# Attention kernel, layer 1: the output projection by seven block products instead of eight, moved within the step

## The chip, the cores and the metric

The kernel runs on one core of one Trainium2 chip. The metric is the device time of one execution in microseconds (us), lower is better; it is given as the median of several executions. The engines are TensorE (PE in the profile, its weight loads PEld), VectorE (DVE), ScalarE (ACT), GpSimd (POOL) and the queue SyncE (SP) that issues the DMAs.

## The reference, cut to what matters

Two attention layers run one after the other over a picture `x` of 128 rows, 256 positions and 256 channels, each with a residual addition. The change concerns layer 1 alone, and in it the last line but one:

```python
# layer 1: x2 is the group-normed picture, one row of 256 positions at a time
qkv = x2 @ w_in.T + b_in                       # 256 -> 768 channels
q, k, v = jnp.split(qkv, 3, axis=-1)           # 4 heads of 64
scores = jnp.einsum('bhid,bhjd->bhij', q, k) / sqrt(64)
scores = jnp.where(|i - j| <= 16, scores, -inf)
attn = softmax(scores)
out = jnp.einsum('bhij,bhjd->bhid', attn, v)
y = out @ w_out.T + b_out                      # the output projection, 256 -> 256
x = x + y
```

## The kernel before

Layer 0 takes the first 1975 us of the profiled execution, layer 1 the rest. Both take the rows in 64 pairs. In layer 1 a pair is an object of class `Pair1`, and one pass of the loop over `p` (L2203) is a step. The order of all work is written out by hand in that loop: each call puts its instructions on the queues of the engines in just this order, and an engine executes its queue in order. A step works on several pairs at once: `now` is pair p, `was` the pair before, `nxt`, `nn` and `n3` are the next three, so that their loads, normalisation and projections run ahead of their attention.

What happens to a pair, with the names that the steps of the prediction use:

- Its rows come from memory in two forms: `xs` for the transposed picture and `xt` for the residual (L1923, L1928, issued on SP three steps ahead). `turn` transposes on DVE (L1936), `centre(k)` normalises on ACT, one call for each of the two halves of the channels (L1941), `add_bias` adds the output bias to `xt` on POOL (L1947).
- Q, K and V of a pair (n = 0, 1, 2) are each a product of two 2 x 2 block matrices: the channels are two halves of 128, and the two rows of the pair are the other index. It is computed by seven block products instead of eight. `mix_weights` forms four combinations of the weight blocks once (L1904 to L1907), `differences` four combinations of the data blocks of each pair on POOL (L1954 to L1957). `product(n, i)` is one of the seven, in the order 1, 2, 6, 5, 7, 4, 3 (L1968). Two PSUM accumulators serve them: x gets products 1, 6, 7, 4 one upon the other, and ACT copies x away after each of them (L1999 for V, L2001 for Q and K); y gets 2, then 5 and 3, and `join(n, i)` on DVE adds to y what ACT had copied (L2008). So a product that adds to x, or starts y anew, waits until x has been copied or y been joined. For V (n = 2) the data block is the stationary operand, and a product is two matmuls of 128 columns; for Q and K it is one matmul of 256.
- `scores(r)` of row r: 16 small matmuls, an exponential on ACT (L2054), and a multiplication by the band mask on POOL (L2056). `apply(r)` multiplies the result `e` by V (L2070) and by ones for the row sums (L2078), split into even and odd key blocks in separate accumulators.
- `copy_sums`, `copy_odd` (ACT, L2089, L2092) and `join_sums`, `join_odd` (DVE, L2095, L2098) bring even and odd together; `invert` takes the reciprocal of the sums (L2101), `weigh` multiplies (L2106) and leaves `oT`, the attention output of a row with channels on partitions; with row 1 it sends the inverted sums to memory (L2111).
- The output projection: `out_block(r, b)` multiplies one block of 128 positions of `oT` by both halves of the channels of `w_out` (L2124), 2 matmuls of 256 columns; a pair has 4 such blocks, 8 matmuls. They land in the second half of each of the two banks of `su_y`, whose first halves hold the row sums. `keep_row(r)` adds the residual `xt` on DVE, straight from PSUM (L2132), and with row 1 sends both rows out (L2140).
- Range checks: `look` queues two pieces for each stretch of 256 values, a maximum (L2160), and a comparison with a minimum (L2157, L2158), all on DVE. `some_checks(n)` takes n pieces from the queue. In most steps before there are two calls of one piece each.

The step before, in short: scores of both rows; application of row 1 of `was`; Q and K products 1, 2, 6, 5, 7; the projection of row 0 of `was`; Q and K products 4 and 3, for Q first, then for K; V products 1 and 2; application of row 0 of `now`; V products 6 and 5; half of the projection of row 1; V product 7; the other half; V products 4 and 3. The inversion and weighting of row 0, the second `centre`, `differences`, `add_bias` and the transposition stand at the end of the step.

```python
self.y = su_y[:, :, 1]
...
self.y[:, b], self.oT[r][:, k, b * P : (b + 1) * P], w_out[:, k, :],
start=(k == 0), stop=(k == KC - 1),
```

Of the kernel before, what the change touches and what calls it, by code (L numbers as in the profile page):

```python
# [9 lines left out]
F32 = mybir.dt.float32  # L10
# [6 lines left out]
P = 128  # L17
# [756 lines left out]
def fast_kernel(  # L774
# [1071 lines left out]
    with tc.tile_pool(name="l1", bufs=2) as sb, tc.tile_pool(  # L1846
# [19 lines left out]
        wst = sb.tile([P, 4, 3, P], F32, name="wst", bufs=1)  # L1866

# [43 lines left out]
        su_y = ps_o.tile([P, 2, 2, I], F32, name="ps_su_y1", tag="su")  # L1911
        su_eo = [su_y[:, n, 0] for n in range(2)]

        class Pair1:
# [53 lines left out]
            def product(self, n, i):  # L1968

                if len(self.ps) == n:  # L1970
                    self.ps.append([mm1("ps_qk", n % 2) for _ in range(2)])
                    self.u.append(sm.tile([P, 3, I], F32, name="u1", tag=f"u{n}", bufs=2))
# [88 lines left out]
            def apply(self, r):  # L2061


                e = self.es[r]
                gap = q0(2) - q0(0)
                for a in range(2):
                    for j in range(NK // 2):
                        for h in range(H1):
                            for k in (2 * j, 2 * j + 1):
                                nc.tensor.matmul(  # L2070
                                    o_eo[k % 2][h * DH : (h + 1) * DH, a, q0(k) : q0(k) + W],
                                    self.v[half(k), r, j, h * D1 + a * DH : h * D1 + (a + 1) * DH],
                                    e[half(k), h % 2, h // 2, j * W : (j + 1) * W], start=True, stop=True,
                                )
                for h in range(H1):
                    for n in range(2):
                        two = su_y[h * DH : (h + 1) * DH, n].rearrange("p a i -> p (a i)")
# [40 lines left out]
            def out_block(self, r, b):  # L2118
                if b == 0:
                    self.y = su_y[:, :, 1]  # L2120
                    if self.p == NP - 1:
                        self.y = mm1("ps_y1", r).rearrange("p (b c) -> p b c", b=NB)
                for k in range(KC):
                    nc.tensor.matmul(  # L2124
                        self.y[:, b], self.oT[r][:, k, b * P : (b + 1) * P], w_out[:, k, :],
                        start=(k == 0), stop=(k == KC - 1),
                    )

            def keep_row(self, r):
                if r == 0:  # L2130
                    self.yo = sb.tile([P, 2 * NB, C], F32, name="yo", tag="yo")
                nc.vector.tensor_tensor(  # L2132
                    self.yo[:, r * NB : (r + 1) * NB, :], self.y,
                    self.xt[:, r * NB : (r + 1) * NB, :], ALU.add,
                )
# [44 lines left out]
        with tc.manual_schedule():  # L2180
# [6 lines left out]
            for t in (*o_eo, su_y):  # L2187
# [14 lines left out]
            was = Nobody()  # L2202
            for p in range(NP - 1):  # L2203
# [14 lines left out]
                now.scores(1)  # L2218
                was.apply(1)
# [28 lines left out]
                nn.centre(0)  # L2248
                some_checks(2 if p > NP - LATE else 0)

                now.apply(0)
                now.copy_sums(0)
# [3 lines left out]
                now.copy_odd(0)  # L2256
                now.join_sums(0)
                was.out_block(1, 0)
                if fast:
                    nxt.product(2, 7)  # L2260
                now.join_odd(0)
                some_checks(2 if p > NP - LATE else p > 0)
                was.out_block(1, 1)
                if fast:
                    nxt.join(2, 5)
                was.keep_row(1)
                if fast:
                    nxt.product(2, 4)
# [4 lines left out]
                nn.centre(1)  # L2273
                nn.differences()
                nn.add_bias()
                n3.turn()
# [3 lines left out]
                was, now, nxt = now, nxt, nn  # L2280

            now.scores(0)
            was.apply(1)
# [106 lines left out]
```

## Time and profile before

| what | us |
|---|---|
| median of 3 executions (3117.92 to 3119.09) | 3118.25 |
| the profiled execution itself | 3119.44 |
| its span, from first to last instruction | 3117.7 |
| of which PE / DVE / ACT / POOL busy | 3016.7 / 2398.7 / 1574.1 / 2267.4 |
| L2124, output projection of layer 1, 1008 records, mean of one | 0.386 |
| L1988, V products, 744 records of the largest group, mean of one | 0.284 |
| L1992, Q and K products, 756 records of the largest group, mean of one | 0.379 |
| L1954, L1955, L1956 / L1957, data differences on POOL | 0.73 / 1.2 |
| L1947, bias addition on POOL, 1024 columns | 2.39 |
| L2132, residual addition on DVE, 512 columns | 0.685 |
| L2008, join on DVE | 0.42 |
| L1999, copy of V's x on ACT | 0.37 |

A group's row in the profile names line, engine and operation, the tiles written and read, shapes and count, then the time the engine was busy with the group and the mean of one in ns, then the idle time ahead of them and who ended it. Matmuls overlap: the mean of one is its latency, while the spacing of their starts says what one costs TensorE. The time line lists instructions in order of start, neighbours of one kind merged into one line with their count; the columns are the start from the span's beginning, the length, the engine, and in brackets, where there are any, the engine's idle time ahead and its releaser.

### The profile page before, as it was taken

The numbers are of one execution on the slowest core, as the hardware profiler recorded it, in microseconds if no ns is written. First come the engines' busy times: TensorE is split into PE (matmuls) and PEld (weight loads), VectorE is DVE, ScalarE is ACT, GpSimd is POOL, SyncE is SP. The second block draws the span as 40 slices with busy tenths as digits, with TensorE's granted clock in tenths as the row PEclk, the third lists the DMA queues.
The fourth block names the chain that finished last, engine by engine and source line by source line (L and its number), as shares of the span: only waits on it lengthen the run. The fifth ranks groups of instructions, "written<-read, shape, count | busy, mean of one in ns | idle before, by whom it ended". The sixth has DMA issues, their size and how long they took to land.

```text
span 3117.7 us, 80605 instructions
## 1 busy us (share of the span) xinstructions
PE 3016.7 (97%) x33642; PEld 2099.2 (67%) x33642; DVE 2398.7 (77%) x4010; ACT 1574.1 (50%) x2639; POOL 2267.4 (73%) x1636
## 2 busy tenths in 40 slices
PE   5689999999999999999999999999999999999998
PEld 4355555566555556555555655688888888888886
DVE  7987777777777777777777777688878777777788
ACT  3454444444444444444444444355555555555554
POOL 3469889889888989888998987455545555555553
PEclk9799999999999999999999999999999999999999
DMA  9952333323332332333233233443434343444431
GB/s 357 390 185 54 97 73 96 100 71 90 91 99 70 99 100 64 93 94 99 69 100 100 63 89 82 116 100 86 101 84 98 90 97 90 95 92 94 94 93 53
DMA packets 690775, 327.90 MB, mean 105 GB/s; under 512 B 538625, under 2 KB 639873, under 8 KB 689249
## 3 DMA queue, kind: packets, MB, share of 16 engines
q1 hardware_dynamic: 686000, 320.02, 38.6%
q8 instruction: 266, 4.36, 0.6%
q10 hardware_dynamic: 4400, 2.63, 0.3%
q14 instruction: 109, 0.88, 0.1%
HBM read 253.83 MB, written 68.74 MB: 103 GB/s over the span
## 4 chain that ended last, share of the span: by engine, by line
PE 91%; DMA 3%; DVE 3%; ACT 1%; POOL 1%; issue 1%; ACTq 0%; SPq 0%; DVEq 0%; POOLq 0%
PE ps_p L1364 21%; PE ps_qk L1992 12%; PE ps_sc L1401 9%; PE ps_ov L1436 7%; PE ps_su_y L2124 7%; PE ps_qk L1988 7%; PE ps_v L1382 7%; PE ps_y L1490 7%; PE ps_o L2070 4%; PE ps_su L1444 3%; PE ps_sc L2045 3%; PE ps_su_y L2078 2%; DMA xa<-in_x_dram 2%; DMA zt<-in_z_dram 1%; DVE st L1199 1%
## 5 line engine op out<-in xcount | busy, mean ns | idle before, releaser
L1425 POOL TENSOR_TENSOR eboth<-e 128x512 f32<-128x512 f32 x512 | 743.5, 1473 | 174.8 <-PE ps_su L1444 95.8
L1421 DVE TENSOR_TENSOR e<-ps_sc,eb 128x1024 f32<-128x1024 f32 x384 | 458.3, 1221 | 288.6 <-ACT ps_sc L1413 288.5
L1413 ACT ACTIVATE ps_sc<-ps_sc 128x1024 f32<-128x1024 f32 x384 | 375.4, 1007 | 435.5 <-PE ps_sc L1401 310.0
L1401 PE MATMUL ps_sc<-qT,kT 32*128 32x256 f32 x4096 | 294.0, 400 | 0.0
L1955 POOL TENSOR_TENSOR dT<-xgT,dT 128x256 f32<-128x256 f32 x63 | 45.9, 729 | 313.5 <-ACT xgT L1941 313.5
L2056 POOL TENSOR_TENSOR e<-e,bw 128x384 f32<-128x384 f32 x256 | 248.1, 1000 | 10.7 <-ACT e L2054 10.7
L2124 PE MATMUL ps_su_y<-w_out,oT 128*128 128x256 f32 x1008 | 254.5, 386 | 0.9 <-DVE sums L2095 0.9
L1401 PEld LDWEIGHTS ps_sc<-qT,kT 32*128 32x128 f32 x4096 | 185.6, 184 | 101.4 <-issue 93.0
L1490 PEld LDWEIGHTS ps_y<-wo,oT 128*128 128x128 f32 x1024 | 194.4, 190 | 81.6 <-issue 43.6
L1436 PE MATMUL ps_ov<-e,v 128*32 128x256 f32 x4096 | 247.6, 382 | 1.1 <-DVE v L1388 1.1
L1364 PE MATMUL ps_p<-xnT,wq 128*128 128x512 f32 x512 | 247.6, 606 | 0.1
L1364 PE MATMUL ps_p<-xgT,wg 128*128 128x512 f32 x512 | 247.3, 605 | 0.0
L1490 PE MATMUL ps_y<-wo,oT 128*128 128x256 f32 x1024 | 242.0, 380 | 1.7 <-POOL oT L1480 1.7
L1382 PE MATMUL ps_v<-wv,xnT 128*128 128x256 f32 x1024 | 241.9, 379 | 0.0
L1364 PE MATMUL ps_p<-xnT,wk 128*128 128x512 f32 x512 | 240.7, 593 | 0.0
L1382 PEld LDWEIGHTS ps_v<-wv,xnT 128*128 128x128 f32 x1024 | 194.6, 190 | 53.9 <-issue 30.9
L2101 DVE RECIPROCAL rv<-sums 128x256 f32<-128x256 f32 x128 | 223.1, 1743 | 0.0
L2001 ACT ACTIVATE u<-ps_qk,bin_c 128x256 f32<-128x256 f32 x378 | 174.3, 475 | 95.0 <-PE ps_qk L1992 95.0
L2124 PEld LDWEIGHTS ps_su_y<-w_out,oT 128*128 128x128 f32 x1008 | 181.9, 190 | 22.3 <-DVE sums L2095 1.3
L1436 PEld LDWEIGHTS ps_ov<-e,v 128*32 128x32 f32 x4096 | 120.2, 110 | 109.2 <-issue 41.4
L1954 POOL TENSOR_TENSOR dT<-xgT 128x256 f32<-128x256 f32 x63 | 46.0, 730 | 184.8 <-ACT xgT L1941 184.8
L1364 PEld LDWEIGHTS ps_p<-xnT,wk 128*128 128x128 f32 x512 | 97.3, 190 | 122.7 <-issue 122.5
(234 smaller groups left out, 6607.1 us busy)
## 6 DMA issues: line engine op xcount, KB each, us to landing
xa<-in_x_dram SPq DMA_DIRECT2D x8, 4096.0 KB
xt<-in_x_dram SPq DMA_DIRECT2D x64, 512.0 KB
x<-xo SPq DMA_DIRECT2D x16, 2048.0 KB
xt<-x SPq DMA_DIRECT2D x64, 512.0 KB
rvb<-rsum SPq DMA_DIRECT2D x252, 128.0 KB
xs<-x SPq DMA_DIRECT2D x252, 128.0 KB
out_dram<-yo SPq DMA_DIRECT2D x63, 512.0 KB
xs<-in_x_dram SPq DMA_DIRECT2D x248, 128.0 KB
```

The source lines that it names most:

```text
L1364: nc.tensor.matmul(ps, w[:, k, m * P : (m + 1) * P], getattr(self, src)[:, k, :], start=(k == 0), stop=(k == KC - 1),)
L1382: nc.tensor.matmul(self.ps_v[:, b * C : (b + 1) * C], self.xnT[:, k, t * P : (t + 1) * P], wv[:, k, :], start=(k == 0), stop=(k == KC - 1),)
L1401: nc.tensor.matmul(self.pss[q // 2][:, q % 2, b, :], self.kT[rs, c, r * I + b * P : r * I + (b + 1) * P], self.qT[rs, c, r * I : (r + 1) * I],
L1413: nc.scalar.activation(self.pss[a], ps, AF.Exp)
L1421: nc.vector.tensor_tensor(es[a], pss[a], eb[:, h : h + 2], ALU.mult)
L1425: nc.gpsimd.tensor_tensor(t, es[a][:, :, 0, :], es[a][:, :, 1, :], ALU.add)
L1436: nc.tensor.matmul(ov[q * D0 : (q + 1) * D0, c, :], self.v[:, r, b, h * D0 : (h + 1) * D0], es[q // 2][:, q % 2, b, :], start=(b == 0), st ...
L1490: nc.tensor.matmul(self.ps_y[:, b * C : (b + 1) * C], self.oT[r][:, k, b * P : (b + 1) * P], wo[:, k, :], start=(k == 0), stop=(k == KC - 1),)
L1992: nc.tensor.matmul(to, lhs, rhs, start=start, stop=True, skip_group_check=True)
L2056: nc.gpsimd.tensor_tensor(e[:, q], e[:, q], bcast(bw.rearrange("p b w -> p (b w)"), 1, KC), ALU.mult)
L2101: nc.vector.reciprocal(self.rv[:, r, :], self.sums)
L2124: nc.tensor.matmul(self.y[:, b], self.oT[r][:, k, b * P : (b + 1) * P], w_out[:, k, :], start=(k == 0), stop=(k == KC - 1),)
```

## The change

- `out_block`'s 8 matmuls of a pair become seven block products of two matmuls of 128 columns each, by the same scheme as Q, K and V: `mix_weights` forms four combinations `wso` of the blocks of `w_out` once, `row_sums` four combinations `oS` of the blocks of `oT` per pair on POOL, `out_product(i)` is a product, with a copy on ACT after 1, 6, 7 and 4 (into `uy`, for 4 straight into the output tile `yo`), `out_join(i)` a join on DVE after 2, 5 and 3. The accumulators are the second halves of two banks, now two tiles.
- The residual is no longer added from PSUM on DVE: `keep_rows` adds `xt` to the whole of `yo` on POOL, one step later (as `old`, two pairs behind `now`), and then sends both rows out.
- The order of the step: all Q and K products 1, 2, 6, 5, 7 run on, and the application of row 0 follows them; then Q and K products 4, 4, 3, 3, then V's seven and the output's seven interleaved in one run. `join_odd(1)` stands ahead of `invert(1)`. The transposition `n3.turn`, `centre(1)`, `differences` and `add_bias` move from the end of the step into or ahead of that run.
- Both pieces of the range checks stand after the last output join, ahead of `invert(0)` and `weigh(0)`; in the late steps two more stand after `row_sums`.
- The buffers `u` of the products go from two to one. The last pair and the one before it keep the old projection; for the one before it the residual addition is split in two.

```diff
+        wso = sb.tile([P, 4, P], F32, name="wso", bufs=1)
...
+            a = [[w_out[:, k, m * P : (m + 1) * P] for k in range(KC)] for m in range(KC)]
+            s1, s2, s3, s4 = (wso[:, n] for n in range(4))
+            nc.gpsimd.tensor_tensor(s1, a[1][0], a[1][1], ALU.add)
+            nc.gpsimd.tensor_tensor(s2, s1, a[0][0], ALU.subtract)
+            nc.gpsimd.tensor_tensor(s3, a[0][0], a[1][0], ALU.subtract)
+            nc.gpsimd.tensor_tensor(s4, a[0][1], s2, ALU.subtract)
...
-        su_y = ps_o.tile([P, 2, 2, I], F32, name="ps_su_y1", tag="su")
-        su_eo = [su_y[:, n, 0] for n in range(2)]
+        su_y = [ps_o.tile([P, 2, I], F32, name=f"ps_su_y{n}", tag=f"su{n}") for n in range(2)]
+        su_eo = [t[:, 0] for t in su_y]
...
+            def row_sums(self):
+
+                self.oS = sb.tile([P, 4, I], F32, name="oS1", tag="oS", bufs=1)
+                b = [[self.oT[r][:, k, :] for r in range(2)] for k in range(KC)]
+                t1, t2, t3, t4 = (self.oS[:, n] for n in range(4))
+                nc.gpsimd.tensor_tensor(t1, b[0][1], b[0][0], ALU.subtract)
+                nc.gpsimd.tensor_tensor(t2, b[1][1], t1, ALU.subtract)
+                nc.gpsimd.tensor_tensor(t3, b[1][1], b[0][1], ALU.subtract)
+                nc.gpsimd.tensor_tensor(t4, b[1][0], t2, ALU.subtract)
+
+            def quarter(self, m, r):
+                return self.yo[:, r * NB : (r + 1) * NB, m * P : (m + 1) * P]
+
+            def out_product(self, i):
+
+                if i == 1:
+                    self.yo = sb.tile([P, 2 * NB, C], F32, name="yo", tag="yo")
+                    self.uy = sm.tile([P, 3, I], F32, name="uy1", tag="uy", bufs=1)
+                x, y = (t[:, 1] for t in su_y)
+                w = lambda m, k: w_out[:, k, m * P : (m + 1) * P]
+                b = lambda k, r: self.oT[r][:, k, :]
+                to, rhs, lhs, start = {
+                    1: (x, w(0, 0), b(0, 0), True),
+                    2: (y, w(0, 1), b(1, 0), True),
+                    6: (x, wso[:, 1], self.oS[:, 1], False),
+                    5: (y, wso[:, 0], self.oS[:, 0], True),
+                    7: (x, wso[:, 2], self.oS[:, 2], False),
+                    4: (x, w(1, 1), self.oS[:, 3], False),
+                    3: (y, wso[:, 3], b(1, 1), False),
+                }[i]
+                for n in range(NB):
+                    at = slice(n * P, (n + 1) * P)
+                    nc.tensor.matmul(
+                        to[:, at], lhs[:, at], rhs, start=start and n == 0, stop=True, skip_group_check=True
+                    )
+                if i in (2, 5, 3):
+                    return
+                if i == 4:
+                    nc.scalar.copy(self.quarter(1, 0), x.rearrange("p (b c) -> p b c", b=NB))
+                else:
+                    nc.scalar.copy(self.uy[:, (1, 6, 7).index(i)], x)
+
+            def out_join(self, i):
+                m, r, at = {2: (0, 0, 0), 5: (1, 1, 2), 3: (0, 1, 1)}[i]
+                y, u = (t.rearrange("p (b c) -> p b c", b=NB) for t in (su_y[1][:, 1], self.uy[:, at]))
+                nc.vector.tensor_tensor(self.quarter(m, r), y, u, ALU.add)
+
+            def keep_rows(self):
+                nc.gpsimd.tensor_tensor(self.yo, self.yo, self.xt, ALU.add)
+                nc.sync.dma_start(rows(out, 2 * self.p, 2), self.yo)
...
                 now.scores(0)
                 now.scores(1)
+                old.keep_rows()
                 was.apply(1)
...
+                was.join_odd(1)
                 was.invert(1)
-                some_checks(p > 0)
                 for i in (6, 5, 7):
                     for n in range(2):
                         nxt.product(n, i)
+                nn.centre(0)
+
+                now.apply(0)
+                now.copy_sums(0)
                 for n in range(2):
                     nxt.join(n, 5)
-                was.join_odd(1)
                 was.weigh(1)
-                was.out_row(0)
+                was.row_sums()
+                some_checks(2 if p > NP - LATE else 0)
+                now.join_sums(0)
                 for n in range(2):
                     nxt.product(n, 4)
+                now.copy_odd(0)
+                for n in range(2):
                     nxt.product(n, 3)
                     nxt.join(n, 3)
+                now.join_odd(0)
                 fast = p < NP - 2
                 if fast:
                     nxt.product(2, 1)
                     nxt.product(2, 2)
                     nxt.join(2, 2)
-                nn.centre(0)
...
+                nn.centre(1)
+                nn.differences()
+                nn.add_bias()
+                was.out_product(1)
+                was.out_product(2)
+                was.out_join(2)
                 if fast:
                     nxt.product(2, 6)
                     nxt.product(2, 5)
...
+                was.out_product(6)
                 if fast:
                     nxt.product(2, 7)
...
+                n3.turn()
+                was.out_product(5)
+                was.out_product(7)
                 if fast:
                     nxt.join(2, 5)
...
+                    nxt.product(2, 4)
+                was.out_join(5)
                 if fast:
...
                     nxt.product(2, 3)
                     nxt.join(2, 3)
+                was.out_product(4)
+                was.out_product(3)
+                was.out_join(3)
+                some_checks(2 if p > 0 else 0)
                 now.invert(0)
                 now.weigh(0)
...
-                was, now, nxt = now, nxt, nn
+                old, was, now, nxt = was, now, nxt, nn
```

More of the change, by code (lines that the diff above doesn't have):

```diff
@@ L1971, in product @@
                     self.ps.append([mm1("ps_qk", n % 2) for _ in range(2)])
-                    self.u.append(sm.tile([P, 3, I], F32, name="u1", tag=f"u{n}", bufs=2))
+                    self.u.append(sm.tile([P, 3, I], F32, name="u1", tag=f"u{n}", bufs=1))
                 x, y = (ps[:, :I] for ps in self.ps[n])
@@ L2076, in apply @@
                     for n in range(2):
-                        two = su_y[h * DH : (h + 1) * DH, n].rearrange("p a i -> p (a i)")
+                        two = su_y[n][h * DH : (h + 1) * DH].rearrange("p a i -> p (a i)")
                         nc.tensor.matmul(
@@ L2119, in out_block @@
                 if b == 0:
-                    self.y = su_y[:, :, 1]
+                    self.y = [t[:, 1] for t in su_y]
                     if self.p == NP - 1:
-                        self.y = mm1("ps_y1", r).rearrange("p (b c) -> p b c", b=NB)
+                        ps = mm1("ps_y1", r)
+                        self.y = [ps[:, n * C : (n + 1) * C] for n in range(NB)]
+                        self.whole = ps
                 for k in range(KC):
                     nc.tensor.matmul(
-                        self.y[:, b], self.oT[r][:, k, b * P : (b + 1) * P], w_out[:, k, :],
+                        self.y[b], self.oT[r][:, k, b * P : (b + 1) * P], w_out[:, k, :],
@@ L2131, in keep_row @@
                     self.yo = sb.tile([P, 2 * NB, C], F32, name="yo", tag="yo")
[L2132 to L2135, printed above, removed]
+                if self.p == NP - 1:
+                    nc.vector.tensor_tensor(
+                        self.yo[:, r * NB : (r + 1) * NB, :], self.whole.rearrange("p (b c) -> p b c", b=NB),
+                        self.xt[:, r * NB : (r + 1) * NB, :], ALU.add,
+                    )
+                for t in range(r * NB, (r + 1) * NB if self.p < NP - 1 else 0):
+                    nc.vector.tensor_tensor(self.yo[:, t, :], self.y[t - r * NB], self.xt[:, t, :], ALU.add)
                 s0 = 2 * self.p
@@ L2186, in fast_kernel @@
                 now.centre(k)
-            for t in (*o_eo, su_y):
+            for t in (*o_eo, *su_y):
                 nc.vector.memset(t, 0.0)
@@ L2200, in fast_kernel @@
             n_eb = cols[0]
-            was = Nobody()
+            old = was = Nobody()
             for p in range(NP - 1):
@@ L2247, in fast_kernel @@
                     nxt.join(2, 2)
-                nn.centre(0)
-                some_checks(2 if p > NP - LATE else 0)
-                now.apply(0)
-                now.copy_sums(0)
+                nn.centre(1)
[4 more added lines that the diff above has]
+                was.out_join(2)
                 if fast:
@@ L2255, in fast_kernel @@
                     nxt.product(2, 5)
-                now.copy_odd(0)
-                now.join_sums(0)
-                was.out_block(1, 0)
+                was.out_product(6)
                 if fast:
                     nxt.product(2, 7)
-                now.join_odd(0)
-                some_checks(2 if p > NP - LATE else p > 0)
-                was.out_block(1, 1)
+                n3.turn()
+                was.out_product(5)
+                was.out_product(7)
                 if fast:
                     nxt.join(2, 5)
-                was.keep_row(1)
+                    nxt.product(2, 4)
+                was.out_join(5)
                 if fast:
-                    nxt.product(2, 4)
                     nxt.product(2, 3)
                     nxt.join(2, 3)
+                was.out_product(4)
+                was.out_product(3)
+                was.out_join(3)
+                some_checks(2 if p > 0 else 0)
                 now.invert(0)
                 now.weigh(0)
[L2273 to L2276, printed above, removed]
                 if p == NP // 2:
@@ L2279, in fast_kernel @@
                     below(n_eb, n_mask, 1e15)
-                was, now, nxt = now, nxt, nn
+                old, was, now, nxt = was, now, nxt, nn
             now.scores(0)
+            old.keep_rows()
             was.apply(1)
```

## The prediction, on record before the result

> **What bounds the kernel now.** I read the page's busy table first, then its chain of waits, then busy time by stretch, then the groups of instructions by shape, and last the order of time inside one step of layer 1.
>
> ```profile
> PE 3016.7 (97%) x33642; PEld 2099.2 (67%) x33642; DVE 2398.7 (77%) x4010; ACT 1574.1 (50%) x2639; POOL 2267.4 (73%) x1636
> ...
> PE 91%; DMA 3%; DVE 3%; ACT 1%; POOL 1%; issue 1%; ACTq 0%; SPq 0%; DVEq 0%; POOLq 0%
> ...
> L2124 PE MATMUL ps_su_y<-w_out,oT 128*128 128x256 f32 x1008 | 254.5, 386 | 0.9 <-DVE sums L2095 0.9
> ```
>
> TensorE carries 91% of the chain that ended last. Busy time in three single steps of layer 1 (columns: stretch, length, then PE, PEld, DVE, ACT, POOL; clock, DMA share, GB/s):
>
> ```profile
> 2400.00:2417.37 17.37, 17.37 (x298) 15.08 (x297) 14.26 (x24) 9.86 (x22) 9.49 (x10) 1.00 0.39 90
> 2600.00:2617.37 17.37, 17.37 (x298) 15.08 (x297) 13.37 (x21) 9.87 (x22) 9.49 (x9) 1.00 0.40 93
> ```
>
> A step takes 17.37 us, and TensorE shows no idle time in it at the full clock. So a step gets shorter by exactly what TensorE is relieved of, as long as nothing new makes it wait. DVE has 3 to 4 us to spare, ACT 7.5, POOL 7.9. A projection is 504 matmuls, and the row counts 1008: each float32 matmul is two records, so a pair has 16.
>
> Order of time in one step (start, length, engine, line, operation):
>
> ```profile
> 2402.10 1.26 PE L1988 MATMUL ps_qk<-w_in,xgT 128*128 128x128 f32 x8
> ...
> 2405.57 1.13 PE L2124 MATMUL ps_su_y<-w_out,oT 128*128 128x256 f32 x4
> ...
> 2406.98 1.03 PE L2124 MATMUL ps_su_y<-w_out,oT 128*128 128x256 f32 x4
> 2407.18 0.37 ACT L1999 COPY u<-ps_qk 128x256 f32<-128x256 f32 x1 [0.99 <-PE ps_qk L1988]
> 2407.58 0.42 DVE L2008 TENSOR_TENSOR v<-ps_qk,u 128x256 f32<-128x256 f32 x1
> 2407.84 0.61 PE L1988 MATMUL ps_qk<-w_in,dT 128*128 128x128 f32 x4
> ...
> 2408.29 0.61 PE L1988 MATMUL ps_qk<-wst,xgT 128*128 128x128 f32 x4
> ...
> 2408.83 1.55 PE L2045 MATMUL ps_sc<-qT,kT 64*64 64x96 f32 x64
> ```
>
> Two things are to be seen. The rate: four records of 256 columns go from 2406.98 to 2407.84, four of 128 columns from 2407.84 to 2408.29. Over all single starts the medians are 216 and 112 ns. And hidden waiting: the eight records at 2402.10 reach the next stage (2403.29) after 1.19 us where eight at 0.112 and the 0.09 of a change of tile shape (2408.29 to 2408.83 is 0.45 + 0.09) make 0.99; there the second V product waited for the join of Q that frees its bank. The four at 2405.57 last 0.96 (next start 2406.53), not 0.86: the load waited for the row sums to leave the bank. That is 0.30 us a step that the busy column doesn't show as idle.
>
> **What the Trainium skill says.** "TensorE: Matmul & The Clock Gate", Back-to-back issue gap, says that in a stream of load and matmul both set the spacing at few columns. The trace agrees: loads last 190 ns each but follow at 112, no slower than the 128-column matmuls, so doubling the loads costs nothing while each can go ahead of its matmul. "SBUF — State Buffer", Practical consequences, says a DVE operation with two SBUF inputs and a POOL operation that reads SBUF exclude each other, and the first to start wins. It agrees: the weighting (L2106) takes 0.69 or 1.25 us, and POOL's L1957 takes 1.24 beside it where L1954 to L1956 take 0.73.
>
> **The change, part by part.** T counts from the start of a step's scores (2408.83 above).
>
> 1. Products. 16 records at 0.216 (3.46) become 7 products of 2 blocks of 2 records, 28 at 0.112 (3.14): minus 0.32 us on the path.
> 2. The two waits. The Q and K products are reordered (both fourths, then both thirds, then V), so V's second product comes 0.43 + 0.45 + 0.22 = 1.10 us after the last record of Q's third start. The join needs 0.42 (matmul start to its end seen by a reader) + 0.42 + 0.05 and the load 0.11 ahead, 1.00: it fits, by 0.1. The first output product now stands 2.7 us after the second application instead of 1.0, with the row sums long joined. Minus 0.30. What is late next is under 5.
> 3. Hand-offs in the new run. Each of x's products 1, 6, 7 is copied by ACT before the next may add to x, and y is read by a join before 5 and 3. From the last record's start: 0.31 to ACT, 0.37 copy, 0.05 back (the V rows above show these), load 0.11 ahead: 0.84. Between lie two products of the other matrix and one of its own steps, 9 × 0.112 = 1.0. So 6 to 7 and 7 to 4, in V and in the output, fit by 0.16; the joins 5, whose addend is product 7's copy, by 0.15. I take 0; the bounds are 0 and, if a load is never ahead, 0.1 plus the lateness for each of six.
> 4. ACT gets 4 copies × 0.37 = 1.5 us: 9.9 to 11.4 of 16.7, hidden. DVE loses two additions (0.685 each), gets three joins (0.42): minus 0.1. The transposition (1.24) moves from T 2.8 to about 13, ahead of the fifth V join, where the copy of product 7 ends later (T 14.5) than it does (14.3): 0. Without that cover, up to 0.2.
> 5. The check pieces (0.28 + 0.42 and 0.36, with starts 1.1 apart in all) were two single places and are now both ahead of the inversion of row 0 (1.74). Queued behind them on DVE: inversion, weighting, sums, then the Q and K joins that products 5 wait for.
>
> ```profile
> 2409.28 1.74 DVE L2101 RECIPROCAL rv<-sums 128x256 f32<-128x256 f32 x1
> 2411.06 0.69 DVE L2106 TENSOR_TENSOR oT<-odd,rv 128x512 f32<-128x512 f32 x1
> 2411.67 1.24 DVE L1936 STREAM_TRANSPOSE xT<-xs 128x1024 f32<-128x1024 f32 x1
> 2412.83 0.39 DVE L2095 TENSOR_TENSOR sums<-ps_su_y,sums 128x256 f32<-128x256 f32 x1
> 2413.27 0.42 DVE L2008 TENSOR_TENSOR qT<-ps_qk,u 128x256 f32<-128x256 f32 x1
> ```
>
> The inversion began at T 0.45, the Q join ended at 4.86, and product 5 has its place at 5.46, so the join may end at 5.3. After: the last output join ends at 0.53, checks to 1.66, inversion to 3.44, weighting 0.69 to 1.46 more (POOL's masks now run beside it, and it may wait for one), sums 0.42, join 0.42: T 5.0 to 5.75. The wait is 0 to 0.45; I take 0.3. Pieces fall in steps 1 to 25 and, late, 57 on; there two more stand ahead of the sums' join, 0.8 in all. Without checks the join ends at 4.8, no wait.
>
> 6. POOL gets the four row sums (4 × 0.73) and the residual of 1024 columns (2.4, as L1947): 9.5 + 5.3 = 14.8, with a collision or two 15.9, of 16.7. Its order closes: weighting of row 1 to T 9.3, row sums to 12.3 (product 6 needs the second at 13.0), differences to 15.2, bias to 17.6, which is T 0.9 of the next step; masks from T 1.4 to 5.4, residual to 7.8. The mask for the moved application is needed at 7.2: three us to spare.
> 7. SP: the output transfer leaves at T 8 of the next step, and the row-sum transfer after it; the loads for the pair three ahead then issue from T 9.5 to 14, some 15 us before the transposition, as now. Priced at nothing; if that cover failed, the landing would be late in each step.
> 8. Once: the moved application of step 0 comes before its masks (done at 2000.4, T 8.9, against T 7.5): 1.5. In the last step V is absent and the hand-offs stand bare: 1.3 less 0.3, near 0.9. Mixing w_out, 4 POOL additions before L1954's 5.8 us of idleness: 0. Two split additions at the end: 0.3.
>
> **Sum.** 31 steps × 0.62 = 19.2; 25 × (0.62 − 0.3) = 8.0; 5 × (0.62 − 0.8) = −0.9; once −2.7: 23.6 us saved. The profiled execution took 3119.44 (span 3117.7 and 1.7 around it), the median is 1.2 below; 3118.25 − 23.6 = 3094.6, so 3094. With no wait in check steps, 61 × 0.62 − 2.7 = 35: 3083; with 0.45 there and 0.1 in half the hand-offs of half the steps, 3107.
>
> **The rivals.** *Late hand-offs.* For it: margins of 0.1 to 0.16 in a row of six, and a wait in V of the same kind exists today. Against it: the V run has held its other hand-offs. Three late by 0.1 each step leave 61 × 0.32 − 8 − 3 − 2.7, about 7: 3111; all six turn it into plus 8, 3126. *POOL becomes the bound,* on the other side. Its place is the ring from the weighting of row 1 over row sums, differences, bias and the next masks; it decides from 16.7 us of POOL work, and makes the kernel slower from 17.37. Its two-input operations would have to be a fifth dearer under DVE's use of the shared reads, 17.8 us: 61 × 0.43, near 27: 3145. For it: 14.8 of 16.7 with up to 0.55 per collision. Against it: only L2106 of DVE's work in a step has two SBUF inputs. *Hidden anyway:* the path then keeps 17.37, 3118; against it, TensorE's lack of any idle time.
>
> **How the numbers follow.** Forecast 0.66; late hand-offs 0.18; POOL 0.13; hidden 0.03. About 0.2% (6.2 us) is what a measurement tells from no change. Of the late hand-offs 0.10 end under 3112, 0.05 within the 0.2%, 0.03 above: faster 0.66 + 0.10 = 0.76, same 0.05 + 0.03 = 0.08, slower 0.13 + 0.03 = 0.16. The range goes from 3079, four under the case without waits (rates are medians), to 3116, well into the late hand-offs.
>
> **What would show it.** Right: a step of 16.75 us without and 17.05 with checks, 28 output records at 0.112, POOL at 15 to 16 us a step with idleness ahead of the row sums, the Q join as the only one TensorE waits for. Wrong: loads of the output products starting late after ACT or DVE in every step (rival 1), POOL without idle time and TensorE waiting for its sums or masks (rival 2). What would make it wrong is a hand-off that takes 0.2 us longer than V's.

## The result, and the profile after

The changed kernel takes **3098.46 us** (median of 4 executions, 3097.95 to 3100.39) beside 3118.6 us for the kernel before on the same chip (3117.92 to 3119.09). The ratio is 0.9939 with a 95% interval of 0.9926 to 0.9951: 20.1 us less, where 24 were forecast. The profiled execution took 3098.43 us; its span is 3096.7.

Busy time, chain by engine, and the queue that brings instructions (packets, MB, share), from the page of the changed kernel:

```profile
PE 2991.3 (97%) x34386; PEld 2088.0 (67%) x34386; DVE 2374.1 (77%) x4075; ACT 1656.8 (54%) x2887; POOL 2587.0 (84%) x1950
...
q8 instruction: 273, 4.47, 0.6%
...
PE 89%; DVE 4%; DMA 4%; POOL 1%; issue 1%; ACT 1%; SPq 0%; ACTq 0%; POOLq 0%; DVEq 0%
```

TensorE still carries the chain. POOL rose from 73% to 84%, as it should. The projection's row is now L2170 (columns: count, shortest, median and longest duration in ns, first and last start, forms):

```profile
L2170 PE MATMUL ps_su_y<-wso,oS x744: 275/275/347, 2022.7 to 3062.0; 128*128 128x128 f32 x186
L2170 PE MATMUL ps_su_y<-w_out,oT x496: 275/275/377, 2020.9 to 3060.0; 128*128 128x128 f32 x166
L2170 PE MATMUL ps_su_y<-w_out,oS x248: 275/275/348, 2025.3 to 3063.2; 128*128 128x128 f32 x124
L2170 PE MATMUL ps_su_y<-wso,oT x248: 275/275/275, 2025.8 to 3063.7; 128*128 128x128 f32 x124
L2170 PEldq EVENT_SEMAPHORE  x186: 51/51/51, 2022.1 to 3062.7; - x186
```

744 + 496 + 248 + 248 is 1736, 28 records for each of 62 steps. The last row will matter: TensorE's sequencer has three waits per step at this line that are instructions of their own. Four single steps by engine (length, then PE, PEld, DVE, ACT, POOL):

```profile
2384.21:2400.95 16.74, 16.74 (x309) 14.85 (x308) 13.73 (x24) 11.19 (x27) 14.18 (x15) 1.00 0.41 96
2485.66:2503.77 18.11, 17.35 (x309) 14.97 (x308) 12.89 (x21) 11.19 (x27) 15.02 (x15) 1.00 0.40 90
2520.52:2538.24 17.72, 17.15 (x309) 14.90 (x308) 12.90 (x21) 11.19 (x27) 14.58 (x15) 1.00 0.40 92
2538.24:2554.98 16.74, 16.74 (x309) 14.85 (x308) 12.91 (x21) 11.19 (x27) 14.62 (x15) 1.00 0.41 96
```

The first step holds check pieces (24 DVE instructions), the others none; it is no longer for that. Plain steps take 16.74 us as forecast, but some take up to 1.7 us more, and in the second row PE itself was idle for 0.76 us.

The time from layer 1's first scores to the end went from 1126.2 to 1105.2 us. By starts of the scores, step by step, the 21.0 us are:

| part | before | after | difference |
|---|---|---|---|
| plain step (median), × 61 | 17.371 | 16.743 | −38.3 |
| steps 1 to 56, sum of what is over the plain step | 5.3 | 16.4 | +11.1 |
| steps 57 to 61, the same | 1.5 | 2.2 | +0.7 |
| step 0 | 14.96 | 16.91 | +1.95 |
| steps 62 and 63 | 20.70 | 21.91 | +1.2 |
| from the last scores to the end | 24.08 | 26.49 | +2.4 |

**Where the second row comes from.** The time line of the changed kernel in the step that begins at 2485.66:

```profile
2493.77 0.27 PEld L2085 LDWEIGHTS ps_su_y<-e,ones 64*32 64x32 f32 x13
...
2495.16 0.51 PE L2085 MATMUL ps_su_y<-e,ones 64*32 64x192 f32 x3 [0.76 <-issue]
```

And its chain of waits there (start, length, what):

```profile
2494.07 0.33 PE ps_su_y L2085 x10
2494.40 0.76 issue
2495.16 0.51 PE ps_su_y L2085 x3
```

TensorE stands for 0.76 us in the middle of an application, between matmuls that need the same data and write the same bank, and the profile names no data that it waited for ("issue"). I call it a **stall** where a recorded instruction of TensorE starts over 0.1 us later after the one before it than at the same place of the median step. Counting TensorE's recorded instructions (622 in each step), the stalls at instruction 273, 271, 269, 267 and 265 of the step fall in steps 3, 10, 17, 24 and 31; three other rows run the same way, seven steps and two instructions apart. 7 × 622 is 17 × 256 + 2. Before, with 595, they are at 264, 271, 278 and 285 in steps 13, 16, 19 and 22, and 3 × 595 is 7 × 256 − 7. Counted through from the first instruction of the execution, all 30 stalls of steps 1 to 56 (16.2 us) stand where the count leaves 193 on division by 256, so they come at whole multiples of 256 instructions from each other. I call such a place a **boundary**.

Before, 9 stalls (5.3 us) stand on boundaries, with the same remainder. Three other steps are late because TensorE waits for a Q join of DVE; the longest of these waits is in step 33, where a comparison of 16 columns on DVE takes 1.86 us beside POOL's bias addition, and the step is 1.06 us longer.

Each stall on a boundary ends 1.2 to 1.6 us after a packet on q8 has ended; such a packet has 16,384 bytes and takes 0.88 to 1.6 us. The Trainium skill ("Runtime: NRT & Kernel Launch", Instruction fetch mechanics) says that instructions are refilled in blocks of 16 KiB, 256 instructions, by the sequencer's own DMA queue while the block before is executed, and calls the cost mostly hidden. The blocks agree with the trace; hidden they are not here. That TensorE waits for its next block of instructions is what I take from this; why the block is late in one order of work and not in another is what most of the experiments ask.

### The profile page after: what moved, and what is told of

Same layout as the page of the kernel before. It is cut to its first block, busy times and chain, and to the rows that moved or that the text cites. A ratio compares the mean times of both kernels' runs of the same rounds, so it can differ in the third digit from the quotient of the medians.

```text
span 3096.7 us, 83063 instructions
## 1 busy us (share of the span) xinstructions
PE 2991.3 (97%) x34386; PEld 2088.0 (67%) x34386; DVE 2374.1 (77%) x4075; ACT 1656.8 (54%) x2887; POOL 2587.0 (84%) x1950
## 4 chain that ended last, share of the span: by engine, by line
PE 89%; DVE 4%; DMA 4%; POOL 1%; issue 1%; ACT 1%; SPq 0%; ACTq 0%; POOLq 0%; DVEq 0%
PE ps_p L1364 21%; PE ps_qk L1999 12%; PE ps_sc L1401 9%; PE ps_ov L1436 8%; PE ps_v L1382 7%; PE ps_y L1490 7%; PE ps_su_y L2170 6%; PE ps_qk L1995 6%; PE ps_o L2077 4%; PE ps_su L1444 3%; PE ps_sc L2052 3%; PE ps_su_y L2085 2%; DMA xa<-in_x_dram 2%; DMA zt<-in_z_dram 1%; DVE st L1199 1%
## 5 line engine op out<-in xcount | busy, mean ns | idle before, releaser
L2063 POOL TENSOR_TENSOR e<-e,bw 128x384 f32<-128x384 f32 x256 | 276.6, 1111 | 77.4 <-ACT e L2061 77.4
L1116 POOL TENSOR_TENSOR zrs<-zrs,mhalf 128x32 f32<-128x32 f32 (+1 forms) x19 | 87.9, 4631 | 114.4 <-DVE zrs L1109 114.4
L1371 ACT ACTIVATE gT<-ps_p,bg_c 128x512 f32<-128x512 f32 x128 | 87.9, 687 | 175.1 <-PE ps_p L1364 175.1
L1999 PE MATMUL ps_qk<-dT,wst 128*128 128x256 f32 x756 | 173.5, 379 | 0.0
L1364 PEld LDWEIGHTS ps_p<-xnT,wq 128*128 128x128 f32 x512 | 91.9, 189 | 114.0 <-issue 112.0
```

The source lines that it names most:

```text
L1364: nc.tensor.matmul(ps, w[:, k, m * P : (m + 1) * P], getattr(self, src)[:, k, :], start=(k == 0), stop=(k == KC - 1),)
L1999: nc.tensor.matmul(to, lhs, rhs, start=start, stop=True, skip_group_check=True)
L2063: nc.gpsimd.tensor_tensor(e[:, q], e[:, q], bcast(bw.rearrange("p b w -> p (b w)"), 1, KC), ALU.mult)
```

## Experiments

A step's **excess** is what is over the median (plain) step of the same run, and excess and stalls are summed over steps 1 to 56. T counts, as in the prediction, from the start of a step's scores. Theory A in the expectations is always that TensorE stands for want of instructions; what it adds about the cause changes from run to run and is told there. Ratios are against the kernel before, beside each run.

**1 and 2. The place of row 0's application.** The change leaves 4.5 us between the end of the first application of a step and the start of the second; before it was about 9.

```diff
 e1: -  now.apply(0), copies and join_sums behind product 7
     +  the same behind the thirds of Q and K; out_product(2) ahead of out_product(1)
 e5: -  for i in (6, 5, 7): products;  now.apply(0)
     +  for i in (6, 5): products;  now.apply(0);  products 7
```

> The application of row 0 is moved 1.7 us later, behind the Q and K fourths and thirds; output product 2 goes ahead of 1, and the second centre ahead of the application, so that the hand-offs still fit. Theory A (TensorE runs out of instructions in the second of two dense bursts, because they now stand 4.4 us apart): the plain step stays 16.74 us, and what the steps 1 to 56 take above it falls from 16 us to 5 to 9 us (before: 5), so about 3090. Theory B (the irregular waits belong to the mixed run of products, or to traffic at fixed intervals, not to where the application stands): the excess stays 14 to 18 us, time within 3 us of 3098.

> The application of row 0 is moved 0.86 us earlier, ahead of the two products 7, so the bursts stand 3.6 us apart. Theory A: the excess of steps 1 to 56 over the plain step grows from 16 us to 20 us or more, the plain step stays 16.74: 3102 or more. Theory B: excess unchanged, time within 3 us of 3098.

Later: 3119.29 us, ratio 1.0006 (0.9997 to 1.0015). The excess fell to 6.8 us, stalls to 21 (9.0 us), 20 of them in the first application. But the plain step rose to 17.27: with nothing between products 7 and 4, the copies of 7 stand bare (twelve records from 6 to 7 take 2.98 us, 2.68 in the changed kernel, and two later stages are 0.1 us longer each). Earlier: 3130.86, ratio 1.0042 (1.0026 to 1.0059), plain step 17.19, and 17.53 where there are check pieces; 16 stalls on boundaries (5.2 us), so no growth, against A's expectation for this run. The distance of the applications alone doesn't set the stalls. Both runs show what the application's place is worth: it is the cover of the Q and K hand-offs.

**3 to 5. Eight products in the new order.** The third has the changed order with the old eight products of 256 columns. The fourth shifts TensorE's instructions by 44 against their blocks. The fifth cuts each of the eight products into two of 128 columns, so that a step has 627 instructions.

```diff
 e2:  -  was.out_product(1) ... was.out_join(3)       (in the run of 18)
      +  was.out_block(0, 0), out_block(0, 1), keep_row(0), out_block(1, 0), out_block(1, 1), keep_row(1)
 e7:  as e2, and in norm1:
      +  for _ in range(11):
      +      nc.tensor.matmul(spare[:32, :16], avg[:, :32], w_in[:, 0, :16], start=True, stop=True)
 e10: as e2, and in out_block:
      +  for n in range(NB):
      +      for k in range(KC): matmul(self.y[b][:, n * P : (n + 1) * P], ..., w_out[:, k, n * P : (n + 1) * P])
```

> The new order of the step is kept, the output projection alone goes back to eight products of 256 columns with the residual added on DVE (no row sums, no POOL residual). Prediction's term: 16 records at 0.216 in place of 28 at 0.112, so the plain step is 16.74 + 0.32 = 17.06 us; with 24 TensorE instructions fewer in a step (598, as before) theory A expects the excess to lie between 5 and 16 us; time 3110 to 3116. Rival: the gain came from the new order alone, then the plain step stays 16.74 and the time is 3098 or less.

> The kernel with the new order and eight output products, which showed no irregular wait in 56 steps, with 11 tiny matmuls (44 TensorE instructions, about 1 us) put ahead of layer 1 and nothing else changed. Its step has about 597 TensorE instructions, and three steps fill seven instruction blocks of 256 almost exactly, so the block borders fall on the same three places of the step throughout; the 44 move them by half their spacing. Theory A' (TensorE runs dry where a block border falls badly against a dense burst): the plain step stays 17.35 us, the excess of steps 1 to 56 rises from 0 to between 5 and 25 us. Rival (the irregular waits come with the seven products): the excess stays 0 to 1, and the time moves by 1 us.

> The changed kernel's order with the old eight block products of the output projection, each of 256 columns cut into two of 128, so 32 records per step in the place of the 16 of the run with eight products, and 627 TensorE instructions per step in the place of 595 (the changed kernel has 622). The plain step is expected at 17.41 us (17.35 of the run with eight products and 32 x 0.112 - 16 x 0.216 = 0.13 more at most). Rival B (the count decides): stalls come back in the applications, 20 or more with an excess of 10 us or more, time about 3128 us. Theory A (other traffic decides) or one in which the pace of a step decides: fewer than 5 stalls, excess under 2 us, time about 3119 us.

Measured: 3115.83 us, ratio 0.9994 (0.9986 to 1.0003); 3115.0, ratio 0.9993; 3123.06, ratio 1.0018 (1.0011 to 1.0025). Plain steps 17.35, 17.36 and 17.47, and **next to no stalls** (excess 0.0, 0.0, 0.1; one stall of 0.11 us in the last of the three, none in the others). The order alone is thus worth little here: of 17.35, 0.33 are the eight products, and 0.28 a wait of this run's own ahead of its third block, which uses up the 0.30 that the order saves. The shift by 44 found no stall, so the first of these runs lacks them by no luck of phase. Its expectation took 597 instructions a step; the trace has 595, so the boundaries move by 7 every three steps even without the shift. And 627 instructions stall less than 595 did before, so the number of instructions doesn't decide either. One step of the fifth run by engine has TensorE busy for 17.45 of its 17.47 us:

```profile
2404.00:2421.47 17.47, 17.45 (x314) 15.37 (x314) 14.14 (x26) 9.81 (x23) 9.63 (x9) 1.00 0.41 92
```

In the waits of layer 1 (total, times, longest) its weight loads wait without a named cause in the applications only once a step, 0.33 us at the start of the second:

```profile
PEld ps_o L2077 <- issue: 19.6, 59, 0.3
```

The same view of the changed kernel has 11 more of these, and 13 at the row sums:

```profile
PEld ps_o L2077 <- issue: 23.7, 71, 0.8
PEld ps_su_y L2085 <- issue: 9.0, 13, 1.4
```

**6. Row 1's application away from the scores.** In the changed kernel the 64 records of score matmuls and the 80 of the application follow each other within 2.8 us, with their loads 288 instructions.

```diff
 now.scores(1)
-was.apply(1)
 nxt.product(0, 1)
 nxt.product(1, 1)
+was.apply(1)
```

> The application of row 1 is moved behind the products 1 of Q and K, so that two slow matmuls of 256 columns each stand between the scores and it (0.86 us); seven products as after the change. Theory A': a burst of 128 and one of 160 instructions no longer run through a block of 256 in 2 us, so the waits in the first application (9.7 us in 24 steps after the change) fall to under 4; those in the second, 7 us in 7 steps, may stay or grow, since the applications now stand 3.5 us apart; time 3089 to 3097. Rival (traffic at fixed times): the excess stays near 16, time 3096 to 3100.

3141.47 us, ratio 1.0078 (1.0062 to 1.0095). No stalls (excess 0.3), in either application, though 622 instructions and their waits are as in the changed kernel. But the plain step is 17.71, with a wait for data in the place of the starving:

```profile
2506.46 1.13 PE L1999 MATMUL ps_qk<-xgT,w_in 128*128 128x256 f32 x4 [0.70 <-ACT e L2061]
```

The product needs the bank that the exponentials of the second scores still read. So density looks like one ingredient: without 288 instructions in a row there is no stall. This run can't tell the breaking up of the stretch from the 0.70 us that TensorE now waits in it, which could be time enough for a block to come. And density isn't the whole, since experiments 3 to 5 have that stretch too.

**7 and 8. Other transfers.** In the changed kernel no data moves at T 1 to 9, where the stalls are, and the row loads run at T 9 to 17; in the runs with eight products they run at T 1 to 9. The seventh leaves out the loads of the turned rows after pair 1; the eighth brings the loads forward.

```diff
 e9:  -  for j in range(P // QB if p else 0):
      +  for j in range(P // QB if p == 1 else 0):      (one tile xs for all pairs)
 e12: +  nc.sync.dma_start(marks[self.p : self.p + 1], self.yo[0:1, NB, :16])    (behind was.out_join(3))
```

> The changed kernel, but the turned rows of layer 1 are loaded once, for pair 1, and used again by every later pair (so the loading of the turned rows of pairs 2 to 63 is left out, and the values of those pairs are not theirs). TensorE's instructions and their order are those of the changed kernel. Theory A (TensorE's instructions arrive by DMA, and these transfers are held up by the row loads that the changed kernel issues beside them): the excess over the plain step in steps 1 to 56 falls from 16 us to under 5, and the time to about 3084 us. Rival B (the row loads have nothing to do with it; the stalls come from how many instructions TensorE takes in how short a time): the excess stays at 14 to 18 us and the time within 3094 to 3100.

> The changed kernel with one more transfer per step: 64 bytes of the product rows go out behind the last join. SP's queue is in order, so the next pair's row loads (1 MB per step), which in the changed kernel follow the output's transfer of the step before at T 9 to 17, now come behind this small transfer, at T 0 to 7, beside TensorE's first application, as in the run with eight products; the output's transfer stays at T 8 to 11. TensorE's instructions and their order are those of the changed kernel. In the changed kernel no transfer of data runs at T 1 to 9, where the stalls are; in the runs with eight products, which have none, the loads run there. Theory C (it is the quiet of the transfers that lets the blocks of instructions come late): the stalls of the first application (24 steps, 9.7 us) go, the excess over the plain step falls from 16 us to under 8, and the time to 3083 to 3091 us. Rival D (the time at which rows are loaded has nothing to do with it): the excess stays at 13 to 18 us, and the time within 3094 to 3102.

3096.88 us, ratio 0.9935 (0.9919 to 0.9952), excess 14.8, 25 stalls on boundaries, 14.0 us; and 3099.14 us, ratio 0.9939 (0.9922 to 0.9956), excess 17.3, 26 such stalls, 17.1 us. The loads did move to T 2 to 8 in the eighth. Neither the absence of the turned rows' loads nor the place of all the row loads touches the stalls; both theories that put them down to other transfers fall. The waits of the eighth in the same view, with line numbers one higher, are those of the changed kernel:

```profile
PEld ps_o L2078 <- issue: 25.4, 72, 0.7
PEld ps_su_y L2086 <- issue: 9.8, 14, 1.2
```

**9. The check pieces apart.** One piece behind invert(1), one behind the last join.

```diff
 was.invert(1)
+some_checks(0 < p <= NP - LATE)
 ...
-some_checks(2 if p > 0 else 0)
+some_checks(2 if p > NP - LATE else p > 0)
```

> The two check pieces of steps 1 to 56 stand apart again, one behind the inversion of row 1, one behind the last output join. Prediction's term (both pieces ahead of the inversion cost 0.3 us in each of 25 steps): the plain step is the same, the time 7 us lower, 3091. What the trace after the change shows (Q's join ends at 4.86 us in a step with checks, as without): the first 25 steps are no shorter, the time within 2 us of 3098.

3096.56 us, ratio 0.9931 (0.9914 to 0.9947). The plain step is 16.743 with pieces and without, as in the changed kernel: their place costs nothing. DVE in a step with pieces in the changed kernel, which begins at 2384.21:

```profile
2384.66 0.41 DVE L2223 TENSOR_REDUCE ok<-sums 128x1 f32<-128x256 f32 x1
2384.99 0.28 DVE L2220 TENSOR_SCALAR above<-sums 128x256 f32<-128x256 f32 x1
...
2385.64 1.74 DVE L2108 RECIPROCAL rv<-sums 128x256 f32<-128x256 f32 x1
...
2387.42 0.81 DVE L2113 TENSOR_TENSOR oT<-odd,rv 128x512 f32<-128x512 f32 x1
...
2388.16 0.41 DVE L2102 TENSOR_TENSOR sums<-ps_su_y,sums 128x256 f32<-128x256 f32 x1
...
2388.65 0.43 DVE L2015 TENSOR_TENSOR qT<-ps_qk,u 128x256 f32<-128x256 f32 x1
```

And the same join in the step without pieces that begins at 2538.24:

```profile
2542.68 0.42 DVE L2015 TENSOR_TENSOR qT<-ps_qk,u 128x256 f32<-128x256 f32 x1 [0.73 <-PE ps_qk L1999]
```

Both start at T 4.44, the second after 0.73 us of idleness in which DVE waits for TensorE's own product. The pieces fill that idleness and end just inside it.

**10. More work for POOL.** One addition of 1024 columns more per step, to nobody's use.

```diff
 nc.gpsimd.tensor_tensor(self.yo, self.yo, self.xt, ALU.add)
+idle = sb.tile([P, 2 * NB, C], F32, name="idle", bufs=1)
+nc.gpsimd.tensor_tensor(idle, self.xt, self.xt, ALU.add)
```

> One more POOL addition of 1024 columns per step beside the residual (2.36 us, result unused), all else as after the change. POOL then has 15.0 + 2.4 = 17.4 us of work in a step of 16.74. If POOL's ring decides from 16.7 us on, as the prediction's rival had it, the step goes to about 17.3, time 3125 to 3140. If POOL's end is not what TensorE waits for, the step stays 16.74 and the time 3098.

3130.65 us, ratio 1.0045 (1.0028 to 1.0062): within the expected time, by another way. The plain step is 17.30, with POOL busy for 16.43 of it, and POOL still waits for the weighting. The time line of POOL in that run:

```profile
2536.62 1.89 POOL L2188 TENSOR_TENSOR idle<-xt 128x1024 f32<-128x1024 f32 x1
2539.20 0.73 POOL L2143 TENSOR_TENSOR oS<-oT,oT 128x256 f32<-128x256 f32 x1 [0.69 <-DVE oT L2113]
```

And that of DVE:

```profile
2537.11 1.95 DVE L2113 TENSOR_TENSOR oT<-odd,rv 128x512 f32<-128x512 f32 x1
```

The weighting, 0.68 us in the changed kernel, takes 1.95 here: it starts beside POOL's addition and ends 0.55 us after it. The Q join behind it on DVE is late for it. In steps without check pieces V's second product waits for that join, and the stage in which V's products begin, 0.89 us in the changed kernel, is 0.53 longer. In steps with pieces the wait is split, 0.37 at product 5 and 0.19 at V's second. POOL hurts by blocking DVE before it is itself full.

**11 and 12. The ends.** The first puts step 0's application behind the thirds and spreads the pieces of the late steps; the second pops six pieces per late step for four.

```diff
 e8:  LATE 8 -> 6;  if not p: now.apply(0) and what follows it, behind product 3
      -  some_checks(2 ...) ahead of now.join_sums(0)
      +  some_checks(1 ...) behind it, and 1 behind n3.turn()
 e11: as e8, with LATE = 8, and
      +  some_checks(2 if p > NP - LATE else 0)      (ahead of was.out_join(5))
```

> The ends of the loop mended, the plain step left as it is: the application of row 0 of step 0 stands behind Q's and K's thirds again; the late checks begin six pairs before the end instead of eight (8 pieces fewer), and of the four pieces of a late step one stands behind the sums' join and one behind the transposition instead of two ahead of the sums' join. Theory: steps 57 to 61 fall by 0.37 each (1.8), the tail by some 2 (26.5 us from its first scores against 24.1 before), step 0 by 1: about 3093. Rival (the tail is longer for the residual on POOL or the split additions): the tail stays at 26.5 and the time at 3096 to 3098.

> The run with mended ends, with six pieces of the check in each of the late steps in the place of four, so that fewer are left for the end. If the pieces left over make the end 2.4 us longer, the time from the last step to the end falls from 26.5 us to 23.5 to 25, and the time to about 3093 us; if they hide behind something else there, it stays at 26.5 and the time at 3095.

3095.21 us, ratio 0.9929 (0.9912 to 0.9945), the least of all runs, 3 us under the changed kernel's median. The intervals of the two ratios overlap, so the gain rests on the traces: step 0 takes 15.72 for 16.91, late steps 16.75 to 16.99 for 17.11 to 17.41; the end stays at 26.56. And 3101.6 us, ratio 0.9952 (0.9936 to 0.9969): the end shrinks to 24.01, what the kernel before had, so the pieces left over are what had made it longer; but late steps take 18.8 to 20.3. The time line of DVE and TensorE in one of them:

```profile
3012.09 2.02 DVE L2220 TENSOR_SCALAR above<-rv 128x256 f32<-128x256 f32 x1
...
3014.95 0.71 PE L2170 MATMUL ps_su_y<-wso,oT 128*128 128x128 f32 x4 [1.83 <-DVE yo L2183]
```

And that of POOL:

```profile
3011.61 2.35 POOL L1954 TENSOR_TENSOR xt<-xt,bout_r 128x1024 f32<-128x1024 f32 x1
```

A comparison that took 0.28 us in the step above takes 2.02 here: it starts beside POOL's bias addition and ends 0.15 us after it, and the join of product 5 stands behind it, 1.83 us of TensorE's time.

## Why the prediction was right, point by point

The time was right, and the mechanism of its two gains; that the sum came out within 4 us is luck: the pieces were priced some 11 us too high, and the stalls, 11 us, not at all.

- **Products and the two hidden waits (1, 2): right.** 0.32 + 0.30 was forecast, the plain step fell by 0.628. By the eight products in the new order, 0.33 of it is the products' own.
- **Hand-offs in the run (3): right.** In the time line the products stand 0.45 or 0.89 us apart, bare multiples of 0.112, with nothing late:

```profile
2601.85 0.61 PE L2170 MATMUL ps_su_y<-wso,oS 128*128 128x128 f32 x4
...
2602.30 0.61 PE L1995 MATMUL ps_qk<-wst,dT 128*128 128x128 f32 x4
...
2602.74 1.06 PE L2170 MATMUL ps_su_y<-wso,oS 128*128 128x128 f32 x8
...
2603.64 0.61 PE L1995 MATMUL ps_qk<-w_in,dT 128*128 128x128 f32 x4
```

- **Check pieces (5): the size was wrong.** In steps 1 to 25 they cost 0, not 0.3, so 7.5 us of loss never came. The step that failed is the collision in the weighting of row 0: by the forecast's own sum a weighting of 0.69 puts the join's end at T 5.0, no wait, and the 0.3 came from letting the masks stretch it to 1.46. It took 0.81. The sum of durations was a little long besides, since many neighbours on DVE overlap by some 0.08 us: the pieces held the queue for 0.98, not 1.13. That is a join at T 4.86, under the 5.0 to 5.75 forecast. The margin is small, and the forecast's fear was not empty: in experiment 2 the same weighting takes 1.22 in steps with pieces, TensorE waits for that join, and such a step is 0.34 longer. In late steps the pieces cost 0.37 rather than 0.8, and there it is one instruction, the comparison beside POOL's row sums:

```profile
2988.72 0.77 DVE L2220 TENSOR_SCALAR above<-rv 128x256 f32<-128x256 f32 x1
```

The Trainium skill ("SBUF — State Buffer", Who interferes with whom) lists `tensor_scalar` among the operations that can take the shared ports, and `tensor_reduce` as one that never contends on this chip. The trace agrees: 0.28, 0.77 and 2.02 for the comparison, 0.41 to 0.42 for the reductions of the changed kernel, of which half run beside POOL. The forecast had applied that section only to operations with two inputs.
- **POOL (6): right on its load** (14.2 to 15.0 us by the windows, 14.8 to 15.9 forecast); as a bound it acts sooner than at full use, through DVE (experiment 10).
- **ACT, DVE, transposition, SP's transfers (4, 7): right at nothing.** Moving the loads by 7 us changed nothing (experiment 8).
- **Once (8): too small.** Step 0 cost 1.95 for 1.5; the last steps cost 1.2, as the 0.9 and 0.3 forecast. The end's 2.4 us were missed: the diff pops four pieces per late step where five were popped before, and the rest runs bare on DVE at the end. DVE from the last weighting to the summary of the pieces, in the changed kernel:

```profile
3083.72 0.69 DVE L2113 TENSOR_TENSOR oT<-odd,rv 128x512 f32<-128x512 f32 x1
...
3088.37 0.17 DVE L2230 TENSOR_SCALAR ok<-ok 128x28 f32<-128x28 f32 x1
```

And in the kernel before:

```profile
3106.60 0.69 DVE L2106 TENSOR_TENSOR oT<-odd,rv 128x512 f32<-128x512 f32 x1
...
3108.85 0.17 DVE L2167 TENSOR_SCALAR ok<-ok 128x28 f32<-128x28 f32 x1
```

From start to start 4.65 us against 2.25.

- **The sums of the rivals: two are off.** Three late hand-offs leave 61 × 0.32 − 8 − 3 − 2.7, which is 5.8 and not 7 (3112 us), and by the same terms six come to about plus 12, not 8. Neither case came.
- **Not in the forecast: the stalls, +11.1 us.** The statement that "a step gets shorter by exactly what TensorE is relieved of, as long as nothing new makes it wait" looked for waits for data alone. Forecast: −37.8 for the steps, +7.5 and +4.0 for pieces, +2.7 once. Measured: −38.3, 0 and +0.7, +5.6, and +11.1 that nobody had priced.

**What stays open.** Shown: the stalls stand on boundaries of 256 instructions and end after an instruction packet; they went in the run that breaks up the dense stretch of scores and application. Shown not to decide: other transfers, and the number of instructions in a step. That the runs with eight products hardly stall is no luck of phase.

The traces show one thing more, how far TensorE has got when a packet starts. Of the packets that start between 1 us before and 0.5 us after the start of a step's scores, the median comes 29 recorded instructions after a boundary in the changed kernel (22 packets) and 20 after it in the kernel before (10), but 18, 31 and 16 ahead of it in the three runs with eight products, counted to the same remainder. With the application moved (experiment 6) it comes 25 after, as late as in the changed kernel, and nothing stalls. As far as these runs go, a stall of the first application takes both, a late packet and a dense stretch.

What makes the packet late is an argument, not shown: that the sequencer has lost its head start. The changed kernel's three separate semaphore waits per step at L2170 don't exist in the eight-product runs. A sequencer held at them would come into the scores with less lead, and ask for its next block later. Against it stands that the kernel before has no such waits in its projection, and its packets are late too and 9 of its boundaries stall, though it has two waits hidden in its run. Removing the three waits alone was not tried.

## What to carry to other kernels

When TensorE is busy without a gap, price a saving by the spacing of its starts and a new hand-off by the last start, the reader's time and the load; that held here to 0.01 us a step. Then ask what a tighter stream of small matmuls does to its own supply of instructions: count them per step, look for "issue" inside a stage that waits for nothing, see whether the places repeat by 256, and compare the start of the instruction packets with the place that TensorE has reached. Fill DVE's idleness with reductions freely, but keep comparisons and two-input operations away from long POOL operations.

## What the runs showed of the hardware that was not expected

- An instruction packet of 16,384 bytes takes 0.88 to 1.6 us, and a stalled TensorE goes on 1.2 to 1.6 us after its end, 2.2 to 2.7 us after its start in the changed kernel; a stretch of 288 instructions there lasts 2.8 us when nothing stalls.
- A 128x256 comparison on DVE takes 0.28 us alone and 2.02 us beside a 1024-column POOL addition; a 128x512 product of two inputs 0.68 and 1.95.
- Cutting 256-column float32 matmuls into two of 128 cost 0.12 us a step for 16 records more (17.35 to 17.47), 7 ns for each.
